# Four graph-attention layers on one core: columns W times a by VectorE, rows R by transfers, the mask without GpSimd

## The chip, the core and the metric

The kernel runs on one core of a Trainium2 chip. The core has five engines with queues of their own: TensorE (PE, with PEld for its weight loads), VectorE (DVE), ScalarE (ACT), GpSimd (POOL) and SyncE (SP), which here only issues transfers (DMA). They share the on-chip memory SBUF; PE writes to eight accumulator banks, the PSUM. An engine runs its queue in order. Where an instruction needs what another engine or a transfer makes, it waits on a semaphore. The metric is the device time of one execution in microseconds, as the median over runs.

## The reference

Input are x of 32 batches x 512 nodes x 256 features, an adjacency matrix adj of 512 x 512 shared by all batches, and the weights of four layers. Each layer adds to x the output of a graph attention over `h = relu(layernorm(x))`. The core of each is

```python
Wh = h @ W
s_i, s_j = Wh @ a1, Wh @ a2
e = leaky_relu(s_i[:, :, None] + s_j[:, None, :], alpha)
e = where(mask, e, -inf)
out = act(softmax(e, axis=-1) @ Wh)
```

Layers 0 and 1 have one head of 256 features (alpha 0.2 and 0.01, then elu or relu); layer 0's mask is `(adj > 0) | eye`. Layer 2 has four heads of 64. Layer 3 is a chain: a linear map from 256 to 512 with relu, an attention over all nodes without a mask (W_fc, 512 features), two elus and a residual, a linear map back to 256, and a masked attention (W_hand) with a residual.

## The kernel before

**The algebra.** With `s = s_i + s_j`, exp(leaky_relu(s)) is max(exp(s), exp(alpha s)). After division by a factor that depends on i alone, which the softmax cancels, the weight of pair (i, j) is exp(s_j) times max(r_i, t_j). r and t are exponentials of the projections scaled by 1 - alpha and alpha - 1. So each weight matrix W gets three more columns: W times a2, and two scaled copies of W times a2 and a1. One product `hT x W` then makes the values and the three exponents. `values` (L669) scales the values by exp(s_j) and leaves the three exponentials in the columns F, F + 1 and F + 2 of v. `weights` (L704) makes w, with j on the partitions and i along the free axis: `max(R, t_j) * maskT`. R is r spread over all partitions: every partition holds the same row r_i, i = 0..511. `averages` multiplies w with v on PE; column F gives the denominator.

**R.** `weights` has two sources for R. By default (L709 to L711), PE makes it: for each of the four tiles of 128 nodes, it turns the column of r, repeated 128 times, against the identity, which leaves R in a PSUM bank. If the caller gives `r`, this is used instead. Layer 2 does that: `rows_out` (L721) turns the four columns of all tiles in one go, ScalarE copies them to an SBUF tile `row`, a transfer puts them into DRAM, and `spread` (L731) reads each row back into all 128 partitions, into one of three buffers `spread`. The sort of layer 3 (`sort_attend`) takes its row in the same way. Layers 0 and 1 and the second attention of layer 3 call `plain` (L749), which uses the default.

**Masked and unmasked attention.** The unmasked attention of layer 3 (`sort_attend`) needs no 512 x 512 weights: nodes are placed in order of t by indirect transfers, running sums are made, and each node gathers the sums at its place. Only the last batch uses the direct form, `attend`.

**Set-up.** x of the first four batches, adj, and all weights come in by transfers from SP. `fetch_w` loads a W with room for three columns, `fetch_a` loads a with one element per partition. `finish_w` then makes the three columns of each 128 rows of W with `project` (L474): PE turns the blocks of W, ScalarE copies them, PE multiplies them with a, VectorE copies the result into W. W0 is done first; the others come from `setup` (L568), a generator, whose steps are placed between those of the first batches. `setup` also makes the mask: VectorE compares adj with 0 into `own`, GpSimd sets the diagonal to 1 with `affine_select` (L572), PE turns the blocks, ScalarE copies them into maskT.

**Order.** The 32 batches run as four streams of eight batches each. Each stream is a Python generator that yields after each piece of work the time at which it wants its next turn (`after_us`); LEAD is the distance between the streams' starts. The order of these turns gives the instructions their ranks. The program is then built twice. The first build is rehearsed: `jobs_of` and `price` give every instruction a duration and `in_order` (L251) lets the engines and SP's queue pick the ready instruction of the lowest rank at every moment. The second build fixes the order found for each engine (`arrange`) and the PSUM banks. So the numbers given to `after_us` are no waits on the chip: they only shift what comes before what.

Of the kernel before, what the change touches and what calls it, by code (L numbers as in the profile page):

```python
# [30 lines left out]
P = 128  # L31
# [36 lines left out]
class Job:  # L68

    def __init__(self, place, ins):  # L70
        self.place, self.ins = place, ins
        self.engine, self.op = str(ins.engine).split(".")[-1], ins.opcode
        self.real, self.soft = set(), set()
        self.after, self.behind, self.opens, self.uses = [], [], [], set()
        self.ready, self.left, self.led, self.rank = 0.0, 0, False, place
# [34 lines left out]
def price(job, outs, ins, in_psum):  # L110

    e, op = job.engine, job.op
    if op == "Matmult":
        (name, _, moving), (_, _, still) = ins[0], ins[1]
        job.span = int(job.ins.tile_size[1])
        turned = name.startswith("ident")
        whole = str(list(job.ins.ins)[1].dtype).endswith("float32")
# [8 lines left out]
    if op == "DMACopy":  # L126
# [6 lines left out]
        if kind == "x" and ins[0][1] == 0:  # L133
            job.took = 5000.0
# [116 lines left out]
def in_order(jobs, users, homes):  # L251
# [27 lines left out]
    array = {"load": 0.0, "flow": 0.0, "end": 0.0, "span": P, "idle": 0.0, "last": 0.0}  # L279
# [23 lines left out]
    def put(job, e, at):  # L303
# [21 lines left out]
        else:  # L325
            clock[e], done = at + job.holds, at + job.took
        array["last"] = max(array["last"], done)
# [71 lines left out]
def fast(ctx, tc, plan, flag, x, adj, w0, a0, w1, a1, w2, a2, mlp1_w, mlp1_b, mlp2_w, mlp2_b,  # L399
# [10 lines left out]
    LEAD = 75.63  # L410
    SLOW = 1.43
    STRETCH = 1.5
# [61 lines left out]
    def project(dst, block, k, a_cols):  # L474
# [12 lines left out]
        nc.vector.tensor_copy(dst, q[:, :n] if len(dst.shape) == 2 else q[:, :n].rearrange("p (h c) -> p h c", c=3))  # L487

    def fetch_w(w, a, name):
# [6 lines left out]
        return t, fetch_a(a, name + "a") if len(a.shape) == 2 else a  # L496

    def finish_w(fetched, alpha):
        t, a_cols = fetched
# [9 lines left out]


    a0_sb = fetch_a(a0, "W0a")
    xts = {0: load_x(0)}
    W0, _ = fetched0 = fetch_w(w0, a0_sb, "W0")
# [4 lines left out]
    W1, _ = fetched1 = fetch_w(w1, a1, "W1")  # L518
# [4 lines left out]
    A2 = const.tile([P, KF, NH * 3], FP, name="A2")  # L523
    nc.vector.memset(A2, 0.0)
    for h in range(NH):
        t, r = divmod(h * D, P)
        for s, c in ((0, 2), (1, 0)):
            nc.sync.dma_start(
                A2[r:r + D, t, h * 3 + c:h * 3 + c + 1],
                a2[h:h + 1, s * D:(s + 1) * D].rearrange("o d -> d o"),  # L530
            )
    A2v = A2.rearrange("p k (h c) -> p (k h) c", c=3)
    WM1 = const.tile([P, KF, H], FP, name="WM1")
    nc.sync.dma_start(WM1, mlp1_w.rearrange("(k p) f -> p k f", p=P))
    WFC, _ = fetched3 = fetch_w(w_fc, a_fc, "WFC")
    WM2 = const.tile([P, KH, F], FP, name="WM2")
    nc.sync.dma_start(WM2, mlp2_w.rearrange("(k p) f -> p k f", p=P))
    WHA, _ = fetched4 = fetch_w(w_hand, a_hand, "WHA")
# [8 lines left out]
    C = F + 2  # L547
# [6 lines left out]
    for _ in finish_w(fetched0, 0.2):  # L554
        pass
# [12 lines left out]
    def setup():  # L568
# [3 lines left out]
        nc.gpsimd.affine_select(  # L572
            out=own, in_=own, pattern=[[P, NT], [-1, N]], base=0, channel_multiplier=1,
            compare_op=OP.not_equal, fill=1.0,
        )
        nc.vector.tensor_reduce(differ[:, 0:1], adj_sb, AX.XY, OP.min)
        nc.vector.tensor_scalar(differ[:, 0:1], differ[:, 0:1], 0.0, None, op0=OP.is_lt)
        for j in range(NT):
# [3 lines left out]
            nc.scalar.copy(maskT[:, j, :], p)  # L582
        yield
        yield from finish_w(fetched1, 0.01)


# [4 lines left out]
        nc.vector.tensor_scalar_mul(A2v[:, :, 1:2], A2v[:, :, 0:1], -0.8)  # L591
        nc.vector.tensor_scalar_mul(A2v[:, :, 2:3], A2v[:, :, 2:3], 0.8)
        for k in range(KF):
            project(W2[:, k, :, D:], lambda k, f: raw2[:, k, f * P:(f + 1) * P], k, A2)
            yield
        yield from finish_w(fetched3, 0.2)
# [17 lines left out]
        yield from finish_w(fetched4, 0.2)  # L614
# [38 lines left out]
    def turned(xn, when):  # L653
# [5 lines left out]
        yield after_us(2.12)  # L659
# [9 lines left out]
    def values(hT, w, rs=None):  # L669

        v = work.tile([P, NT, F + 3], FP, tag="v", name="v", bufs=4)
        for t in range(NT):
# [14 lines left out]
            if t + 1 < NT:  # L687
                yield after_us(0.72)
        yield after_us(0.03)
        return v  # L690

    def linear_t(inT, w, bias, name, bufs):
# [3 lines left out]
        for f in range(ft):  # L696
# [4 lines left out]
            yield after_us(0.76 if f == ft - 1 else 1.59)  # L701
# [47 lines left out]
    def plain(hT, w, rs=None):  # L749
        v = yield from values(hT, w, rs)  # L750
        wt = weights(lambda t: v[:, t, F + 2:F + 3], lambda j: v[:, j, F + 1:F + 2])
        note(v[:, :, F:])
        yield after_us(4.32)
# [19 lines left out]
    def layer0(xt, xn, rs, when):  # L773
        v, wt = yield from plain((yield from turned(xn, when)), W0)
        xn, rs = new_xn(), small([NT], "rs")
        for t0 in range(0, NT, 2):
            r, q = pair(), pair("q")
            for i in range(2):
# [3 lines left out]
                if i == 0:  # L782
                    yield after_us(2.78)
            add_elu(xt[:, t0:t0 + 2, :], r, q)
            norm(xt, xn, rs, t0, True)
            last, when = when, after_us(1.15)
            if t0 == 0:
                yield after_us(5.01)
# [3 lines left out]
    def layer1(xt, xn, rs, when):  # L792
        v, wt = yield from plain((yield from turned(xn, when)), W1, rs)
        xn, rs = new_xn(), small([NT], "rs")
        for t0 in range(0, NT, 2):
            r = pair()
            for i in range(2):
                p, rd = averages(v, wt, t0 + i)
                nc.scalar.activation(r[:, i, :], p, AF.Relu, scale=rd)
                if i == 0:  # L800
                    yield after_us(2.38)
# [3 lines left out]
            last, when = when, after_us(4.67)  # L805
            if t0 == 0:
                yield after_us(12.63)
# [3 lines left out]
    def layer2(xt, xn, rs, when):  # L811
        hT = yield from turned(xn, when)
        v = work.tile([P, NT, NH, CH], FP, tag="v", name="v2", bufs=4)
        for t in range(NT):
# [11 lines left out]
            yield after_us(0.87 if t + 1 < NT else 0.62)  # L826
# [4 lines left out]
        def begin():  # L831
# [4 lines left out]
            return after_us(1.36)  # L836
# [7 lines left out]
        yield after_us(9.98)  # L844
        begin()
        note(v.rearrange("p t h c -> p (t h) c")[:, :, D:])
        yield after_us(7.5)
        when = begin()
        for g, parts in enumerate(plan):
# [10 lines left out]
            yield after_us(0.16)  # L860
# [29 lines left out]
            yield after_us(0.3)  # L890
# [3 lines left out]
        yield after_us(9.4)  # L894
        return xn, rs, after_us(1.32)
# [28 lines left out]
    def attend(oT, b):  # L924

        halves, ends = fc_values()
        for c in range(2):
            for t in range(NT):
                project_half(oT, halves, ends, c, t)
                yield after_us(0.3)  # L930
# [4 lines left out]
        yield after_us(0)  # L935
        ys = []
        for t in range(NT):
# [10 lines left out]
            yield after_us(0.16)  # L948
            if t:
                mlp_in(oT, ys[t - 1], t - 1)  # L950
                yield after_us(0.3)
        yield after_us(3.15)
        mlp_in(oT, ys[-1], NT - 1)
        yield after_us(2.72)

    def sort_attend(oT, b):
# [6 lines left out]
        for t in range(NT):  # L963
            project_half(oT, halves, ends, 0, t)
            yield after_us(0.49)
        project_half(oT, halves, ends, 1, 0)
        yield after_us(0.06)
# [3 lines left out]
        yield after_us(0.73)  # L971
# [10 lines left out]
        sort = after_us(16.48)  # L982
        yield after_us(7.62)
        for t in range(1, NT):
            project_half(oT, halves, ends, 1, t)
            yield after_us(1.52)
# [7 lines left out]
        for c in range(2):  # L994
# [17 lines left out]
            sort = after_us(1.66)  # L1012
        places = table[:N, :].rearrange("(p t) (k c n) -> p (t k) c n", t=NT, k=2, c=2)
        sort = after_us(6.05)
        for c in range(2):
# [15 lines left out]
            yield after_us(3.52)  # L1031
# [602 lines left out]
```

## Time and profile before

| what | value |
|---|---|
| median of 11 runs | 2784.43 us (2781.42 to 2793.45) |
| the profiled execution | 2787.69 us, its span 2785.8 us |
| busy PE / DVE / ACT / POOL | 2742.5 / 2272.2 / 1635.5 / 521.4 us |
| mean granted clock of PE | 0.994 of full speed |
| transfers | 287.37 MB, mean 103 GB/s |
| issues of `spread<-row` and `row<-row` | 159 of 256 KB and 63 of 2 or 8 KB |
| turns `b<-ident,v` | 416 (384 of them for R, 32 for layer 2's rows) |

A line of the page such as `L714 DVE SCALAR_TENSOR_TENSOR w<-spread,v,maskT` names the source line, the engine, the operation, and what it writes and reads by the program's names; `b` is a PSUM bank, `spread` the SBUF buffer of R. In a fp32 product PE needs two instructions; a turn against the identity needs one. In a timeline, the first number is the start in us from the span's beginning, the second the length of the merged group, and the bracket gives the idle time before it and what ended it.

### The profile page before, as it was taken

The numbers are of one execution on the slowest core, as the hardware profiler recorded it, in microseconds if no ns is written. First come the engines' busy times: TensorE is split into PE (matmuls) and PEld (weight loads), VectorE is DVE, ScalarE is ACT, GpSimd is POOL, SyncE is SP. The second block draws the span as 40 slices with busy tenths as digits, with TensorE's granted clock in tenths as the row PEclk, the third lists the DMA queues.
The fourth block names the chain that finished last, engine by engine and source line by source line (L and its number), as shares of the span: only waits on it lengthen the run. The fifth ranks groups of instructions, "written<-read, shape, count | busy, mean of one in ns | idle before, by whom it ended". The sixth has DMA issues, their size and how long they took to land.

```text
span 2785.8 us, 41668 instructions
## 1 busy us (share of the span) xinstructions
PE 2742.5 (98%) x14316; PEld 1953.9 (70%) x14316; DVE 2272.2 (82%) x5834; ACT 1635.5 (59%) x4142; POOL 521.4 (19%) x515
## 2 busy tenths in 40 slices
PE   7999999999999999999999999999999999999998
PEld 6676676767766677766866667776676766867665
DVE  4779887897978879788796888978888897888964
ACT  3455666556655666556655566655666555655555
POOL 0012221121202222022211222111221122211220
PEclk8999999999999999999999999999999999999999
DMA  3024341343413434134331433223432233422430
GB/s 99 16 75 135 108 141 65 98 136 98 149 51 111 137 107 134 35 123 130 116 117 52 132 120 124 92 69 115 130 118 89 84 127 103 141 80 84 134 118 32
DMA packets 202499, 287.37 MB, mean 103 GB/s; under 512 B 18156, under 2 KB 157350, under 8 KB 202280
## 3 DMA queue, kind: packets, MB, share of 16 engines
q1 hardware_dynamic: 172520, 186.34, 21.4%
q0 software_dynamic: 29760, 98.30, 10.5%
q8 instruction: 114, 1.87, 0.3%
q14 instruction: 105, 0.86, 0.1%
HBM read 169.14 MB, written 115.45 MB: 102 GB/s over the span
## 4 chain that ended last, share of the span: by engine, by line
PE 88%; DVE 4%; issue 4%; DMA 2%; ACT 1%; POOL 1%; SPq 0%; POOLq 0%; ACTq 0%
PE b L430 66%; PE b L434 12%; PE b L438 10%; DMA spread<-row 1%; DVE st L630 0%; DVE w L714 0%; DVE y L771 0%; DMA row<-row 0%; DVE xn L637 0%; DMA W<-in_L_gnn_W_dram 0%; POOL order L998 0%; DVE y L1107 0%; DVE y L764 0%; DMA g<-table,at 0%; DVE q L769 0%
## 5 line engine op out<-in xcount | busy, mean ns | idle before, releaser
L430 PE MATMUL b<-v,w 128*128 128x257 f32 (+1 forms) x3136 | 767.7, 383 | 2.1 <-DVE w L718 1.0
L430 PEld LDWEIGHTS b<-v,w 128*128 128x128 f32 x3136 | 573.4, 191 | 123.1 <-issue 34.2
L430 PE MATMUL b<-WFC,oT 128*128 128x256 f32 (+1 forms) x2048 | 490.5, 381 | 1.0 <-ACT oT L700 1.0
L430 PEld LDWEIGHTS b<-WFC,oT 128*128 128x128 f32 x2048 | 374.2, 189 | 75.2 <-issue 18.6
L430 PE MATMUL b<-W,hT 128*128 128x259 f32 (+1 forms) x1536 | 397.3, 389 | 0.5 <-ACT hT L651 0.5
L714 DVE SCALAR_TENSOR_TENSOR w<-spread,v,maskT 128x512 f32<-128x512 f32 x512 | 373.1, 778 | 13.6 <-PE b L434 13.1
L434 PE MATMUL b<-w,v 128*32 128x512 f32 x3072 | 349.4, 595 | 0.0
L998 POOL DMA_INDIRECT order<-v,at x248 | 262.2, 1057 | 411.4 <-DVE at L980 147.0
L430 PEld LDWEIGHTS b<-W,hT 128*128 128x128 f32 x1536 | 280.0, 192 | 61.8 <-issue 22.7
L714 DVE SCALAR_TENSOR_TENSOR w<-b,v,maskT 128x512 f32<-128x512 f32 x384 | 264.7, 743 | 21.9 <-PE b L438 19.6
L1110 POOL TENSOR_TENSOR x<-x,y 128x512 f32<-128x512 f32 x62 | 82.4, 1328 | 1030.9 <-ACT y L1108 1021.7
L1052 POOL DMA_INDIRECT g<-table,at x124 | 139.7, 1127 | 568.2 <-DMA table<-sums 270.6
L430 PE MATMUL b<-hT,WM 128*128 128x512 f32 x512 | 243.6, 592 | 0.4 <-ACT hT L651 0.4
L434 PEld LDWEIGHTS b<-w,v 128*32 128x32 f32 x3072 | 89.8, 109 | 198.2 <-issue 195.6
L430 PE MATMUL b<-oT,WM 128*128 128x512 f32 x512 | 227.5, 592 | 0.0
L630 DVE BATCH_NORM_STATS2 st<-x 128x6 f32<-128x256 f32 x512 | 194.3, 408 | 4.9 <-DMA x<-in_x_dram 3.6
L651 ACT ACTIVATE hT<-b 128x512 f32<-128x512 f32 x256 | 147.6, 593 | 45.1 <-PE b L438 45.1
L746 DVE RECIPROCAL rden<-b 128x1 f32<-128x1 f32 x388 | 57.7, 160 | 137.5 <-PE b L430 134.9
L430 PEld LDWEIGHTS b<-oT,WM 128*128 128x128 f32 x512 | 97.1, 190 | 102.8 <-issue 100.0
L438 PE MATMUL b<-ident,xn 128*128 128x128 f32 x1024 | 158.2, 276 | 8.2 <-DVE xn L637 8.2
L771 DVE TENSOR_TENSOR y<-q,y 128x512 f32<-128x512 f32 (+1 forms) x194 | 132.5, 683 | 33.1 <-ACT q L770 31.9
L922 ACT ACTIVATE v<-b,ends 128x256 f32<-128x256 f32 x256 | 120.6, 471 | 62.9 <-PE b L430 50.4
(154 smaller groups left out, 4237.1 us busy)
## 6 DMA issues: line engine op xcount, KB each, us to landing
table<-sums SPq DMA_DIRECT2D x62, 1032.0 KB
spread<-row SPq DMA_DIRECT2D x159, 256.0 KB
sums<-order SPq DMA_DIRECT2D x62, 516.0 KB
x<-in_x_dram SPq DMA_DIRECT2D x32, 512.0 KB
out_dram<-x SPq DMA_DIRECT2D x62, 256.0 KB
sums<-order SPq DMA_DIRECT2D x62, 129.0 KB
order<-v,at POOLq DMA_INDIRECT x248, 2.7
g<-table,at POOLq DMA_INDIRECT x124, 5.0
```

Of the source, the lines that this page charges most:

```text
L430: nc.tensor.matmul(p, w, x, **flags)
L434: nc.tensor.matmul(p, w, x, tile_position=(0, c), **flags)
L438: nc.tensor.transpose(p, x, i)
L630: nc.vector.bn_stats(st[:, i, :], xt[:, t0 + i, :])
L651: nc.scalar.activation(hT[:, :, t0 * P:(t0 + 2) * P], p.rearrange("p (k n) -> p k n", k=KF), AF.Relu)
L714: nc.vector.scalar_tensor_tensor(wt[:, j, :], r, t_col(j), maskT[:, j, :], op0=OP.max, op1=OP.mult)
L746: nc.vector.reciprocal(r, den)
L771: nc.vector.tensor_tensor(r, q, r, op=OP.add)
L922: nc.scalar.activation(halves[c][:, t, :F], ps[:, :F], AF.Copy, scale=ends[:, t, 0:1])
L998: one = nc.gpsimd.indirect_dma_start(out=orders[c], out_offset=bass.IndirectOffsetOnAxis(ap=at[:, 0, t:t + 1], axis=0), in_=halves[c][:, t ...
L1052: nc.gpsimd.indirect_dma_start(out=g, out_offset=None, in_=table, in_offset=bass.IndirectOffsetOnAxis(ap=at[:, 1, t:t + 1], axis=0),)
L1110: (nc.gpsimd if n == 2 else nc.vector).tensor_tensor(xr, xr, y, op=OP.add)
```

## The change

Four things change together.

1. Columns W times a. W0 keeps `finish_w`. For W1, WFC and WHA, a is spread over all partitions by one transfer each (`fetch_row`), and VectorE multiplies each row of W with it and adds up along the row (`finish_by_rows`); the scaling of two of the columns is done on GpSimd on W's own columns. W2 gets its columns by a product and a reduction per head. The transfers of single elements of a1, a2, a_fc and a_hand go, and the order of the first transfers becomes x, W0, a0, adj.
2. R. `plain` gets `far`; layers 0, 1 and layer 3's second attention make R with `rows_out` and `spread`, as layer 2 does, from column F + 2 of v.
3. The mask. `affine_select` goes. After each bank of turned blocks is copied to maskT, VectorE writes the diagonal block once more as the maximum of the turned block and the identity.
4. The order. `price` and `in_order` treat the first loads as sharing one pipe (`flux`), and turns no longer count as a switch of PE's tile size. LEAD, SLOW, STRETCH and nearly all times given to `after_us` are new, PAUSES adds pauses after layers 0 to 2 of each stream's first batch, and the steps of `setup` are placed 19.61 apart and not 1.5.

```diff
-        job.span = int(job.ins.tile_size[1])
         turned = name.startswith("ident")
+        job.span = P if turned else int(job.ins.tile_size[1])
...
-        if kind == "x" and ins[0][1] == 0:
-            job.took = 5000.0
+        if ins[0][0].startswith("in_") and not (kind == "x" and ins[0][1] >= 4 * 512 * 256):
+            job.took, job.flux = 2500.0, max(160.0, 4.0 * elements(s) * s[0][1] / 350.0)
...
-    LEAD = 75.63
-    SLOW = 1.43
-    STRETCH = 1.5
+    LEAD = 81.69
+    GO = 7.0
+    PAUSES = (1.98, 20.79, 0, 9.87, 13.42, 5.98, 12.87, 2.43, 0, 28.8, 13.7, 0)
+    SLOW = 1.53
+    STRETCH = 1.75
...
+    def finish_by_rows(t, row, alpha):
+
+        kt, halves = t.shape[1], row.shape[1] // (2 * F)
+        for k in range(kt):
+            dots = work.tile([P, 2, 2], FP, tag="T", name="dots", bufs=2 * NS)
+            for s, c in ((0, 2), (1, 0)):
+                for i in range(halves):
+                    at = (s * halves + i) * F
+                    junk = work.tile([P, N], BF, tag="junk", name="junk0", bufs=1)[:, :F]
+                    nc.vector.scalar_tensor_tensor(
+                        junk, t[:, k, i * (F + 3):i * (F + 3) + F], 1.0, row[:, at:at + F], op0=OP.mult, op1=OP.mult,
+                        accum_out=t[:, k, F + c:F + c + 1] if halves == 1 else dots[:, s, i:i + 1],
+                    )
+                if halves > 1:
+                    nc.vector.tensor_tensor(t[:, k, F + c:F + c + 1], dots[:, s, 0:1], dots[:, s, 1:2], op=OP.add)
+            yield
+        scale_a(t[:, :, F:F + 3], alpha)
...
+    def fetch_row(a, dst):
+        nc.sync.dma_start(dst, a.partition_broadcast(P))
+        return dst
...
-    for h in range(NH):
-        t, r = divmod(h * D, P)
-        for s, c in ((0, 2), (1, 0)):
-            nc.sync.dma_start(
-                A2[r:r + D, t, h * 3 + c:h * 3 + c + 1],
-                a2[h:h + 1, s * D:(s + 1) * D].rearrange("o d -> d o"),
-            )
...
         nc.vector.tensor_scalar(own, adj_sb, 0.0, None, op0=OP.is_gt)
-        nc.gpsimd.affine_select(
-            out=own, in_=own, pattern=[[P, NT], [-1, N]], base=0, channel_multiplier=1,
-            compare_op=OP.not_equal, fill=1.0,
-        )
...
             nc.scalar.copy(maskT[:, j, :], p)
+            nc.vector.tensor_tensor(maskT[:, j, j * P:(j + 1) * P], p[:, j * P:(j + 1) * P], ident, op=OP.max)
...
-    def plain(hT, w, rs=None):
+    def plain(hT, w, rs=None, far=False):
         v = yield from values(hT, w, rs)
-        wt = weights(lambda t: v[:, t, F + 2:F + 3], lambda j: v[:, j, F + 1:F + 2])
+        r = None
+        if far:
+            r = spread(rows_out(v[:, :, F + 2], 1)[0, :])
+            yield after_us(11.34)
+        wt = weights(lambda t: v[:, t, F + 2:F + 3], lambda j: v[:, j, F + 1:F + 2], r=r)
         note(v[:, :, F:])
-        yield after_us(4.32)
+        yield after_us(0.41)
...
-    ready = {i: i * LEAD + late for i, late in enumerate((0, -2.47, -0.73, -8.03))}
+    ready = {i: i * LEAD + late for i, late in enumerate((0, 4.35, 4.97, 5.59))}
...
-    ready[NS] = 0.35
+    ready[NS] = 1.42
...
-            ready[i] += 1.5
+            ready[i] += 19.61
```

## The prediction

> **What bounds the kernel now.** I read the page's busy shares first, then busy time by stretch, then PE's timeline, and the chain of waits last. The page and two stretches (columns: length, then busy time of PE, PEld, DVE, ACT, POOL, PE's clock, DMA share, GB/s):
>
> ```profile
> PE 2742.5 (98%) x14316; PEld 1953.9 (70%) x14316; DVE 2272.2 (82%) x5834; ACT 1635.5 (59%) x4142; POOL 521.4 (19%) x515
> ...
> PE 88%; DVE 4%; issue 4%; DMA 2%; ACT 1%; POOL 1%; SPq 0%; POOLq 0%; ACTq 0%
> ```
>
> ```profile
> 0.00:60.00 60.00, 40.12 (x190) 34.05 (x191) 22.92 (x78) 20.11 (x51) 5.71 (x18) 0.83 0.40 115
> ...
> 516.29:853.42 337.13, 336.97 (x1770) 239.86 (x1769) 284.06 (x728) 203.38 (x517) 66.38 (x65) 1.00 0.34 108
> ```
>
> From 516.29 on, the program repeats every 337.13 us, one round of four batches, and PE is busy for 336.97 of it. So a round is worth what PE's own instructions take, and no wait of another engine shows. Room lies only in the first 60 us (PE busy 40, clock 0.83) and in the end (PE's last instruction starts at 2777.1 of 2785.8).
>
> PE's timeline, start and length. Lengths overlap, so I take the distance between starts:
>
> ```profile
> 1025.80 0.60 PE L438 MATMUL b<-ident,v 128*128 128x128 f32 x4
> 1026.23 0.60 PE L438 MATMUL b<-ident,rT 128*128 128x128 f32 x4
> ...
> 1034.07 0.27 PE L438 MATMUL b<-ident,ends 128*4 128x128 f32 x1
> 1034.18 1.90 PE L430 MATMUL b<-v,w 128*128 128x257 f32 x8
> ```
>
> The first row is what the change removes: the four turns that make R, 0.43 us, 0.109 each. The third is what it puts there: one turn of a few columns, 0.11. The same view of the start:
>
> ```profile
> 6.98 0.66 PE L438 MATMUL b<-ident,W 128*128 128x128 f32 x2 [6.98 <-DMA W<-in_L_gnn_W_dram]
> ...
> 19.46 2.82 PE L438 MATMUL b<-ident,own 128*128 128x128 f32 x12 [4.21 <-POOL own L572]
> ...
> 30.38 0.44 PE L438 MATMUL b<-ident,raw 128*128 128x128 f32 x2 [2.30 <-DVE W L487]
> 30.65 0.60 PE L438 MATMUL b<-ident,v 128*128 128x128 f32 x4
> ...
> 32.10 2.08 PE L430 MATMUL b<-v,w 128*128 128x257 f32 x4
> ...
> 53.97 1.11 PE L438 MATMUL b<-ident,xn 128*128 128x128 f32 x4 [3.84 <-DVE xn L637]
> ```
>
> At present R is ready for VectorE within 32.10 - 30.65 = 1.45 us of its first turn. The price of R by transfers is in the chain of waits, where the sort's own row takes this way:
>
> ```profile
> 359.94 0.25 ACT row L726
> 360.19 0.02 issue
> 360.20 2.75 DMA row<-row
> 362.96 0.02 issue
> 362.97 4.90 DMA spread<-row
> ```
>
> **The change part by part.** The sum is made against the profiled execution: span 2785.8, 2787.69 in all, 3.3 above the median 2784.43 (0.12%). I take the difference and put it on the median. A measurement of this kernel can tell about 0.2% (5.6 us) from no change.
>
> (a) R of layers 0 and 1 and of layer 3's second attention. Each of 32 batches loses 3 x 4 turns and gains 3 x 1: 32 x 9 x 0.109 = 31.4 us of PE. PE bounds the rounds, so this is worth all of it, if nothing else stops PE: -31.4.
>
> (b) Columns W times a. On PE, the turns and small products of W1, raw2, WFC and WHA stand between 23.80 and 50.13. By distances of starts: W1 1.55, raw2 with A 1.80, WFC 5.95, WHA 1.63, together -10.9. VectorE gets them: 24 products of 128x256 with accumulation (as 128x258, 484 ns, and an accumulator read, 84) and 4 pairs of about 0.84 us, 17 us. VectorE is busy 22.9 of the first 60 us, so most lies in its idle time.
>
> (c) Waits that go. The mask no longer passes POOL, and `own` no longer stands behind the copy of raw2 on VectorE's queue: adj is there by about 9.6 (issue 2.88, own transfer some 6.7), and the walk below has PE reach `own` with no gap: 4.21. The 2.30 before raw2's turns go with these turns, as does 0.52 before WHA's last product. x and W0 are issued before the 256 single elements of each half of a0, W0 at 1.3 and not at 2.33: 1.0. Together -8.0. The four `max` on the diagonal blocks (0.3 us each) run beside PE's next turns. SP loses 14 of its small early issues and gains four spreads of a.
>
> (d) What the first R costs. In the changed program's order PE has nothing between stream 0's turn of r and its first average: cover 0.11 us. Walk: PE starts at 5.95; the W0 steps and xn's turns end at about 12.2 (as 6.98 to 13.20 now); values and `own`, about 9 us at a clock partly halved, end near 21; ACT's last scaling and the turn, 22.5. But SP issues in order, and the row stands behind all weights and an x of 512 KB. SP's issues that wait for x1, x2 and x3 stand at 11.4, 12.6 and 14.1 now: 1.35 us for 512 KB. After x3 come 3.75 MB up to WHA, 10 to 11 us, so WHA lands near 25, and the row waits for its semaphore. Row 2.75, spread 4.0 to 4.9, first w 0.74: averages begin near 33.5, against 32.10 now. PE waits some 11 us there, then starts at half clock: the four products at 32.10 took 2.08 now, 0.87 at full rate. No setup stands between them, so the averages end near 43, and layer 1's values near 56, against 61.5. Its R has a cover of 3.7 us, need about 6.8 to 8.4, so PE waits 3 to 5 more and layer 1's averages begin at 64 to 66, against 63.74, with 3 us more of stream 1 done. Of the 19.6 us that (b), (c) and two R's save by then, some 18 are given back: +18 (12 to 24).
>
> (e) The rest of the run-in, to 265. Stream 1's first R has a cover of 3.6 and hides behind the wait before it; layer 2's four rows 8.6, which must bring two heads (VectorE 4 x 0.744 for the first); the others 8.3 to 15.6. The lower bound is no loss, the upper 2 us for each of five: +4 (0 to 10).
>
> (f) The rounds. By the changed order and the row prices, PE's cover from each turn of r to the first product that needs it is 9.28, 9.28, 9.50, 10.09 and so on to 13.18 us, twelve in a round. The need: 0.5 to 1 until ACT's copy, 0.25, row 1.2 to 4, spread 3 to 4.9 (the chain showed 2.75 + 4.90 and, at 2046, 3.72 + 4.04), first w 0.74: 6 to 9.7, plus VectorE's queue. Mostly hidden; +4 over all rounds, bounds 0 and 30 (a third of a microsecond for each of 84 steady R's). SP gets 12 rows and 12 spreads more per round, 24 issues of about 0.35 us beside some 75, and 3.1 MB beside 36: it can be held up, not filled. ACT gets 12 copies of 0.25.
>
> Now w is made from SBUF and not from PSUM; the tile's view:
>
> ```profile
> L714 DVE SCALAR_TENSOR_TENSOR w<-spread,v,maskT x512: 720/744/2142, 98.7 to 2651.2; 128x512 f32<-128x512 f32 x171
> L714 DVE SCALAR_TENSOR_TENSOR w<-b,v,maskT x384: 727/743/752, 31.3 to 2769.8; 128x512 f32<-128x512 f32 x192
> ```
>
> The medians are equal; only the SBUF form has a tail (mean 778 against 743), so 384 x 35 ns = 13.4 us more on VectorE, 1.7 in a round where it idles 53: nothing on the path. The Trainium skill speaks against this part: "GPSIMD Engine Reference", section Specifications, says that GpSimd's SBUF interfaces are shared with VectorE, with contention where an instruction has two SBUF inputs, which this form has and the PSUM form has not. By that rule, the 62 additions of x on POOL (1328 ns each) could each hold one w up to the tail's 1.4 us: an estimate of 87 us of VectorE at the worst, 11 in a round, still inside its 53. The sum stays as the rows have it.
>
> A second page prices (f) otherwise. "DMA: Bandwidth & Descriptors", section Anatomy of one DMA, gives some 2.0 us plus bytes over 436 GB/s for a transfer, fitted on GpSimd's path: an estimate of 4.6 us for row and spread together, which would make (f) zero and the forecast 4 us lower. The chain measured 7.65 and 7.76 us for the two, and I keep to that.
>
> (g) The end. The last two R's have covers of 7.1 and 7.9 against some 6.8; PE's gaps there come from layer chains that stay: +1 (-2 to +5).
>
> Sum: -31.4 - 10.9 - 8.0 + 18 + 4 + 4 + 1 = -23.3, so 2784.4 - 23.3 = 2761.
>
> **The rivals.** 1. All covered: (d) at 12, the rest nothing, -38, 2746. For it: the rounds of now, where each R by transfer in layer 2 is waited for by nobody. Against: those have more work in between, and the first R is plainly uncovered. 2. A longer run-in: (d) and (e) at their upper ends and (g) at 5 give -7.3, 2777, and one more stretch at half clock (6.8 us in the records) 2784. For it: 53.97 above, where one wait is followed by PE at half clock. 3. Slower: R by transfers becomes the rounds' bound. If transfers take so much longer that the chain from turn to w takes 10.7 us, the four shortest covers lack 4.6 us per round, 32 over seven, and 4 of these are in (f): 2789. That is the point from which it decides; at 12 us eight covers lack 13 per round, 92 in all: 2849. Against: 9.7 is the worst sum of the rows shown. For it: SP's order, where a row waits behind whatever stands before it. 4. VectorE as the bound: 284 + 2 in a round of 333 is 86%, no bound by itself.
>
> **How the numbers follow.** Forecast (2750 to 2771) 0.60; rival 1 0.18; rival 2 0.13, of which half ends within 0.2%; rival 3 and 4 together 0.09. Faster by over 0.2% is 0.60 + 0.18 + half of rival 2, 0.85; within 0.2% 0.07; slower 0.08, the rest of 3 being a draw. The range runs from rival 1's lower edge to where rival 2 ends: 2742 to 2783.
>
> **What would show it.** Right: a round of about 333.2 with PE busy but for 0.5; no turns b<-ident,v of 128 columns; no PE wait on POOL own; a PE gap of about 10 us near 22 to 33, ended by DVE w, with SP's row issue at 25 or later; stream 0's layer 1 averages at 63 to 66. Wrong: (f), if PE's gaps in a round end on DVE w behind DMA spread; (d), if the row goes out well before 25, or if PE's waits sit elsewhere; (a), if the turns' time comes back as gaps.

## The result and the profile after

The changed kernel takes 2767.0 us (median of 8 runs, 2762.41 to 2770.82) against 2784.45 us of the kernel before beside it: a ratio of 0.9935, 95% interval 0.9926 to 0.9943. It is 17.4 us faster; 23.3 were forecast. The profiled execution has a span of 2766.3 us, 19.5 less than before's 2785.8.

The page of the changed kernel, busy time and the chain that ended last:

```profile
PE 2708.6 (98%) x13944; PEld 1908.4 (69%) x13944; DVE 2290.4 (83%) x5889; ACT 1627.3 (59%) x4228; POOL 517.1 (19%) x516
...
PE 68%; DVE 24%; ACT 5%; issue 1%; DMA 1%; SPq 0%; POOL 0%; DVEq 0%; POOLq 0%
```

PE is still busy for 98%, but the chain of waits that ended last now runs through VectorE for a quarter of the span, where it was 4%. That is a warning more than a loss: PE and VectorE now hand work to each other with little in hand, as the run with a longer way for the row shows below.

The first 60 us and one round, by stretch (columns as before):

```profile
0.00:60.00 60.00, 34.09 (x133) 27.59 (x134) 33.92 (x133) 20.38 (x57) 4.04 (x16) 0.80 0.45 143
785.72:1120.54 334.82, 334.03 (x1734) 235.36 (x1733) 285.21 (x730) 203.03 (x529) 65.33 (x64) 1.00 0.37 118
```

A round went from 337.13 to 334.82 us, with PE busy for all but 0.8 of it. In the first 60 us PE does less (34 us and not 40), partly because work was removed, partly because it waits. PE's timeline shows where:

```profile
19.54 0.27 PE L442 MATMUL b<-ident,v 128*4 128x128 f32 x1 [0.26 <-ACT v L703]
33.60 10.21 PE L434 MATMUL b<-v,w 128*128 128x257 f32 x32 [13.79 <-DVE w L737]
...
48.73 0.66 PE L442 MATMUL b<-ident,xn 128*128 128x128 f32 x2 [3.55 <-ACT rs L656]
```

The single turn of r ends at 19.8, and the first average starts 13.79 us later. The chain of waits through that gap (start, length, what):

```profile
16.47 9.25 DMA WHA<-in_L_gnn_W_hand_dram
...
25.79 3.54 DMA row<-row
29.33 0.02 issue
29.35 3.42 DMA spread<-row
32.77 0.02 issue
32.79 0.76 DVE w L737
```

ScalarE had copied the row by 20.1. It went out only at 25.79, when a load issued long before it, WHA of layer 3, had landed.

### The profile page after: what moved, and what is told of

It is laid out like the page before. It is cut to its first block, busy times and chain, and to the rows that moved or that the text cites. A ratio compares the mean times of both kernels' runs of the same rounds, so it can differ in the third digit from the quotient of the medians.

```text
span 2766.3 us, 41413 instructions
## 1 busy us (share of the span) xinstructions
PE 2708.6 (98%) x13944; PEld 1908.4 (69%) x13944; DVE 2290.4 (83%) x5889; ACT 1627.3 (59%) x4228; POOL 517.1 (19%) x516
## 4 chain that ended last, share of the span: by engine, by line
PE 68%; DVE 24%; ACT 5%; issue 1%; DMA 1%; SPq 0%; POOL 0%; DVEq 0%; POOLq 0%
PE b L434 54%; PE b L438 7%; DVE w L737 7%; PE b L442 7%; DVE st L653 2%; DVE sums L1055 1%; DVE y L798 1%; DVE sums L1070 1%; DVE xn L664 1%; ACT q L797 1%; DVE xn L660 1%; DVE y L1134 1%; DVE sums L1063 1%; DVE y L791 1%; DVE g L1093 1%
## 5 line engine op out<-in xcount | busy, mean ns | idle before, releaser
L434 PEld LDWEIGHTS b<-v,w 128*128 128x128 f32 x3136 | 579.2, 191 | 145.1 <-issue 30.6
L737 DVE SCALAR_TENSOR_TENSOR w<-spread,v,maskT 128x512 f32<-128x512 f32 x896 | 652.8, 761 | 26.3 <-DMA spread<-row 25.7
L434 PE MATMUL b<-WFC,oT 128*128 128x256 f32 (+1 forms) x2048 | 504.7, 381 | 0.0
L434 PE MATMUL b<-W,hT 128*128 128x259 f32 (+1 forms) x1536 | 386.1, 388 | 0.8 <-ACT hT L674 0.8
L442 PE MATMUL b<-ident,xn 128*128 128x128 f32 x1024 | 161.8, 279 | 12.4 <-DVE xn L660 6.8
L442 PEld LDWEIGHTS b<-ident,xn 128*128 128x128 f32 x1024 | 122.7, 141 | 62.1 <-DVE xn L660 13.5
L1137 POOL TENSOR_TENSOR x<-x,y 128x512 f32<-128x512 f32 x62 | 86.1, 1388 | 357.5 <-ACT y L1135 355.1
```

The costliest lines, as they stand in the source:

```text
L434: nc.tensor.matmul(p, w, x, **flags)
L442: nc.tensor.transpose(p, x, i)
L737: nc.vector.scalar_tensor_tensor(wt[:, j, :], r, t_col(j), maskT[:, j, :], op0=OP.max, op1=OP.mult)
L1137: (nc.gpsimd if n == 2 else nc.vector).tensor_tensor(xr, xr, y, op=OP.add)
```

## The experiments

Two notes on reading. Chips fall into two levels: on some the kernel before takes 2784 us, on others 2815 to 2817. Every ratio is therefore to the kernel before on the same chip, and differences are told within one level. And a kernel's order is written anew for every edit, since it is found by a rehearsal of the whole program; an edit in one place can move instructions everywhere.

Theory 1: R by transfers earns the gain in the rounds, and the run-in gives part of it back. Theory 2: R by transfers brings new small waits through VectorE into every round. Theory 3: the gain is that of the set-up, or of the order, and R adds nothing.

| kernel | median us | before, same chip | ratio, 95% interval |
|---|---|---|---|
| order and set-up new, R by turns | 2813.87 | 2814.87 | 0.9995 (0.9983 to 1.0006) |
| set-up alone | 2811.28 | 2814.87 | 0.9983 (0.9972 to 0.9994) |
| order alone | 2814.00 | 2814.87 | 0.9994 (0.9983 to 1.0005) |
| changed kernel, second level | 2772.40 | 2817.07 | 0.9839 (0.9822 to 0.9855) |
| kernel before, profiled there | 2816.76 | 2817.07 | 0.9998 (0.9988 to 1.0007) |
| R by transfers alone | 3103.09 | 2817.07 | 1.1013 (1.0995 to 1.1032) |
| first batch's R by turns | 2953.46 | 2817.07 | 1.0483 (1.0464 to 1.0502) |
| changed kernel, first level again | 2762.45 | 2783.81 | 0.9919 (0.9905 to 0.9932) |
| R's row by a longer way | 2817.76 | 2783.81 | 1.0122 (1.0107 to 1.0138) |
| first R a constant | 2757.56 | 2783.81 | 0.9905 (0.9890 to 0.9921) |
| late loads behind the first row | 2757.82 | 2783.81 | 0.9904 (0.9889 to 0.9920) |
| all of layer 3's loads behind it | 2777.12 | 2817.18 | 0.9854 (0.9841 to 0.9868) |

### One part at a time: set-up, order, both without R

The first kernel is the changed one with R made by PE again:

```diff
-        v, wt = yield from plain((yield from turned(xn, when)), W0, far=True)
+        v, wt = yield from plain((yield from turned(xn, when)), W0)
```

(the same for W1 and WHA).

> The changed kernel, but R of layers 0, 1 and layer 3's second attention made on PE by turns again; the rest of the change, the new order times included, stays. Theory 1 (R by transfers takes 3.93 us per round off PE and gives about 20 us back in the run-in; the 1.6 us of small PE waits that a round of the changed kernel has belong to the new order times, not to R): rounds of 334.82 + 3.93 = 338.7 us, PE's wait of 13.8 us near 20 gone, total 2767 + 31.4 - 20 = 2778. Theory 2 (the small waits come with R by transfers, through VectorE): rounds of 337.1, total 2767 to 2769. Theory 3 (the gain is of the set-up alone and R by transfers gains nothing net): total 2767 or less.

The second is the kernel before with parts 1 and 3 of the change and the new sequence of loads, but R by turns and the old times; the third is the kernel before with part 4 alone.

> The kernel before with the new set-up alone (columns W times a on VectorE, spread a, mask without GpSimd, new order of the first loads); R by turns and the order times of before. Theory 1: rounds stay at 337.1; the run-in saves PE's 10.9 us of set-up and 8.0 us of waits, most of it on the path because nothing now waits for R: 2784.4 - 15 = 2769 (2765 to 2775). Theory 3: the same 2767 as the whole change. If the set-up were hidden by streams anyway: 2780 to 2784.

> The kernel before with the new order alone (prices of first loads and turns, LEAD, PAUSES, all times given to after_us); set-up and R as before. Theory 1 (the small PE waits of 1.6 us per round come with the new order): rounds of 338.5 to 338.8, total 2784 + 11 = 2795 or a little more in the run-in. Theory 2 (they come with R by transfers): rounds of 337.1, total 2782 to 2790. If the new order is itself better: below 2780.

Against the kernel before they measured -1.0, -3.6 and -0.9 us, on a chip of the second level. None brings the gain, nor do set-up and order together, so theory 3 falls there; on the first level the three were not run. The set-up takes 9.3 us of full-speed work off PE and three waits, and 3.6 came out: in its start PE waits 9.03 us at 25 us for the first w and 3.70 for `own`. The kernel with set-up and order but R by turns has later rounds of 338.9 us on average (theory 1 had 338.7), with 1.9 us of PE waits in each; the changed kernel on a chip of this level (next section) has 1.0. The small waits are thus no smaller without R by transfers, which speaks against theory 2; each order has its own.

### The changed kernel and the kernel before on a chip of the second level

> The changed kernel once more, beside the runs below on one chip. Theory 1 (R by transfers earns the gain, about 3.9 us of every round of four streams, and the run-in gives some 9 back): about 17 us below the kernel before, as measured first (2767.0 against 2784.4), whatever the level of the chip. Theory 3 (set-up or order earn it, and R by transfers is paid for by new waits): on a chip where set-up alone was worth 3.6 us and order with set-up 1.0, no more than some 5 us below.

> The kernel before, profiled on this chip, to hold its rounds against those of the runs beside it. Same time as the kernel before; rounds of 337.1 us if the chip is as the first one; if the level is 30 us higher as with the last three runs, the difference should be found in the rounds (about 4 us in each) as slips of ScalarE and VectorE with a half-speed clock window, not in TensorE's work.

The gain is 44.7 us there, not 17.4. From the first kernel above (-1.0, on another chip of this level) to the changed one (-44.7) only R changes, and the order that follows from it. The turns explain 31.4 of this; the rest is not settled to the microsecond, since the orders differ and the changed kernel's profiled run (2782.14) was the slowest of its four.

Why is the gain larger there? The kernel before loses time in each round at one place. PE's one long wait in a round on this chip, and the chain that leads to it in the same round (start, length, what):

```profile
PE b L430 <- DVE oT L1125: 2.4, 1, 2.4
```

```profile
924.32 0.60 DVE y L764
924.92 2.88 another core or an unknown queue
927.81 0.02 issue
927.83 0.70 DVE oT L1125
```

ScalarE stands still over the same time (2.63 us before `v<-b,ends`, L922), also released by something that the profile doesn't name. On the first chip the same two instructions follow with no gap. This costs 2.4 us of PE's time per round, and its rounds are 340.8 to 342.4 us where they were 337.13. The changed order has this wait once (3.61 us from 239.55) and not in the later rounds, which are 335.8 us on average. What releases the two engines late on such chips stays open; indirect transfers of GpSimd are under way there, and nothing was tried on them.

### R by transfers alone

```diff
+        if far:
+            r = spread(rows_out(v[:, :, F + 2], 1)[0, :])
+            yield after_us(20.0)
```

with `far=True` in the three calls, in the kernel before. (The pause is 20.0 and not the change's 11.34: with that one and the other times of before, the three buffers of R allowed no order, and no kernel came of it.)

> The kernel before with R by transfers alone: set-up, mask and all order times of before, except that the order's pause between the row's transfer and the weights is 20.0 us. The turns give 3.9 us in each round. Its order leaves some R's in each round only 1.6, 4.6 and 6.6 us between their last turn and the first use, others 16 and more, where the chain of row and spread took 10 us. Theory 1: waits of about 8, 6 and 4 us per round take the gain and more: rounds about 8 to 14 us longer, some 60 to 100 us above the kernel before. Rival (the hidden transfers are shorter in a round than in the run-in, or the wait falls on VectorE only): within 20 us of the kernel before.

It is 286 us slower, 10%. One round, PE's waits in a round, and PE's timeline at the largest:

```profile
1045.62:1424.60 378.98, 351.12 (x1740) 242.04 (x1739) 288.48 (x736) 205.35 (x532) 67.38 (x64) 0.96 0.34 106
```

```profile
PE b L430 <- DVE w L714: 7.8, 4, 6.8
PE b L438 <- DVE y L775: 6.1, 5, 2.6
PE b L430 <- ACT y L1101: 3.2, 1, 3.2
PE b L438 <- DVE xn L641: 2.7, 3, 1.6
```

```profile
1173.14 0.27 PE L438 MATMUL b<-ident,v 128*4 128x128 f32 x1
1180.18 8.64 PE L430 MATMUL b<-v,w 128*128 128x257 f32 x30 [6.78 <-DVE w L714]
```

The last turn of r stands right in front of the averages, so 6.78 us of its chain lie bare. That is the wait that theory 1 foresaw, but the waits for w are only 7.8 us of a round. Waits on y, xn and oT make up more than half of the 29.7 us of waits per round, and 28.2 us of each round run at half clock (the 0.96), which costs 14 more. 29.7 + 14.1 - 4.0 for the turns is 39.8; the round is 41.8 longer than the 337.13 of the first chip. The expected 60 to 100 us counted the bare R's alone. It missed that the four streams had moved: their distances at the same step are 54, 65, 65 and 196 us in this kernel, and 68, 72, 65 and 137 in the kernel before. That these distances cause the other waits is likely, but no run tests it. So taking the turns off PE gains nothing by itself: it depends on the order. The run does not price R by transfers in the old order, because that order was not kept.

### The first batch's R by turns

```diff
-    def layer0(xt, xn, rs, when):
-        v, wt = yield from plain((yield from turned(xn, when)), W0, far=True)
+    def layer0(xt, xn, rs, when, far):
+        v, wt = yield from plain((yield from turned(xn, when)), W0, far=far)
```

with `far` true from batch 1 on, and the same for layer 1.

> The changed kernel, with R of the first batch's layers 0 and 1 by turns on TensorE as before; all the rest as changed. 64 turns come back on TensorE (64 by 0.109 us, 7.0 us), and the first wait of TensorE for w (13.8 us, with a clock window of 17.1 us at half speed behind it, some 8 us lost) loses its cause. Theory 1, in which the run-in's waits for R cost 18 us: 13.8 + 1.2 + up to 8 less 7.0, so 8 to 16 us below the changed kernel. Rival: the run-in is bound by the start-up chain of VectorE and ScalarE that stands behind the wait (xn, rs, the masks), so that other gaps take its place: within 4 us of the changed kernel, either way.

Both expectations were wrong: 136 us above the kernel before, some 181 above the changed one. The 13.79 us wait is gone, but PE waits 41.6 us in the run-in in all (39.6 in the changed kernel on this chip), in smaller pieces: 3.78 on rs, 2.37 on xn, 5.76 on w, 4.22 on xn. The streams then stand 76, 83, 90 and 107 us apart, where the changed kernel has 79, 71, 110 and 75, and later rounds take 353 to 361 us. So the edit changed the whole order, and this run does not price the first wait; a later one does. A stretch of one, with PE's clock in the third number from the end, and the instruction in front of it:

```profile
1047.70:1061.40 13.70, 10.52 (x28) 7.19 (x29) 8.06 (x22) 8.48 (x18) 1.92 (x2) 0.50 0.39 116
```

```profile
1047.79 1.11 PE L442 MATMUL b<-ident,y 128*128 128x128 f32 x4 [2.98 <-issue]
```

A wait of 2.98 us is followed by 13.7 us at half clock, in which two more waits lie, of 1.39 and 1.17 us. The Trainium skill, "TensorE: Matmul & The Clock Gate", section "HAM oscillation — how this bites in real kernels", gives as the rule that PE should have no idle gap above some 3.4 us. This case disagrees in the unsafe direction: 2.98 was enough here, and waits of 1.6 to 2.2 us were enough in the kernel of the last section. It was not certain either: of eight waits of 2.4 us in the kernel before on this chip, three were followed by a half-speed window of 3.4 us and five by none. A wait of 3.7 us near 89 us in the changed kernel was followed by such a window on two chips and by none on a third.

### R's row by a longer way

```diff
-            r = spread(rows_out(v[:, :, F + 2], 1)[0, :])
+            near = rows_out(v[:, :, F + 2], 1)
+            way = dram.tile([1, N], FP, tag="way", name="way", bufs=4)
+            nc.sync.dma_start(way, near)
+            r = spread(way[0, :])
```

The rehearsal prices the added transfer at nothing, so the order on PE, VectorE and ScalarE is that of the changed kernel. This and the next two kernels ran beside the changed kernel on a chip of the first level.

> The changed kernel, but R's row of layers 0, 1 and the hand layer goes through DRAM once more (a 2 KB transfer from DRAM to DRAM between row and spread); the order on TensorE, VectorE and ScalarE is that of the changed kernel. A row transfer took 1.14 to 4.3 us, so each of the 96 chains, 7.2 us long in the middle and 9.8 in the longest tenth, grows by about 2 us. Theory 1 (R is hidden in the rounds, but with covers of only 9.3 to 13.2 us, so with 1 to 3 us in hand): the three waits of the run-in grow by 2 each, and the longest chains of a round overrun the shortest covers by up to 2.5 us in one to three places: 10 to 40 us above the changed kernel, with new TensorE waits that end on w. Rival (the covers counted in TensorE's work understate what is in hand): no wait for w in the rounds, 3 to 7 us above it from the run-in alone.

> The changed kernel, for comparison on the same chip: 17 us (as measured first) to 45 us (as measured on the second chip) below the kernel before.

The kernel is 55.3 us slower than the changed one beside it (2817.76 against 2762.45): more than the 10 to 40 of theory 1, and far more than the rival's 3 to 7. PE's longest waits over three rounds, here and then in the changed kernel beside it:

```profile
PE b L434 <- DVE w L737: 8.6, 8, 2.2
PE b L442 <- ACT y L889: 1.2, 3, 0.5
```

```profile
PE b L442 <- DVE xn L660: 1.0, 3, 0.3
PE b L442 <- DVE y L798: 0.3, 1, 0.3
```

These three rounds take 1026.1 us against 1004.1. Of the 22.0 us, 8.6 are the waits for w, of which the changed kernel has none in a round; 6.9 are averages that start one by one, as w comes; the rest is in smaller waits and slips. VectorE waits for a spread nine times in a round, and not three. The run-in is 6.7 us longer, with PE's first two waits for w at 15.48 and 3.00 us for 12.11 and 1.27. So the rival falls, and theory 1 has the place right and the price too low: R is hidden in the rounds with less in hand than one more small transfer takes (from its issue to the spread's, this one took 1.9 us in the middle of 96). The prediction's third rival had 4.6 us per round if the chain took 10.7 us and 13 if it took 12; this run lies between.

### The price of the first wait

```diff
-            r = spread(rows_out(v[:, :, F + 2], 1)[0, :])
+            row = rows_out(v[:, :, F + 2], 1)[0, :]
+            if begin:
+                r = work.tile([P, N], FP, tag="spread", name="first", bufs=3)
+                nc.gpsimd.memset(begin.pop() and r, 1.0)
+            else:
+                r = spread(row)
```

The rehearsal is told that this tile comes when the spread would, so PE, ScalarE and GpSimd keep their order. R of batch 0's layer 0 is left out of the computation.

> The changed kernel with its order on every engine kept, but R of batch 0's layer 0 is a constant tile, set at the start by GpSimd, instead of the row's values (so this R is left out of what is computed, and one spread transfer with it). Prices the first wait of TensorE (13.8 us, end at 33.6) by itself. VectorE then reaches the first w after the products that wait for the last layer's vector (landed at 23.5), near 25.1 in place of 32.8. Theory 1 (the wait and the half clock behind it are lost time, the 18 us of the prediction): the wait shrinks to 5 to 7 us, the half clock's 17.1 us to 10.2 or less, and the kernel is 7 to 12 us below the changed kernel. Rival (the wait covers the start-up of VectorE and ScalarE, which would end the next waits instead): within 3 us of it.

It measured 4.9 us below the changed kernel (2757.56 against 2762.45; each ratio is known to about 4 us): between theory 1 (7 to 12) and the rival (within 3). The traces show more. PE's first averages, in the changed kernel beside it and here:

```profile
33.50 9.42 PE L434 MATMUL b<-v,w 128*128 128x257 f32 x32 [12.11 <-DVE w L737]
```

```profile
26.89 9.08 PE L436 MATMUL b<-v,w 128*128 128x257 f32 x32 [5.29 <-DVE w L739]
```

The wait falls from 12.11 to 5.29 us; what is left of it is VectorE's products for W_fc, which stand before w and wait for a vector until 24.65. The half clock behind it falls from 13.7 to 6.8 us. At the end of the run-in, taken at stream 3's first layer 2 row (the turn of 16 columns), this kernel is at 266.25 us and the changed one at 275.22. So 9.0 us were lost time, as theory 1 has it, and no other gap took their place; the later rounds are alike (334.8 and 334.7 us). The spans of the two profiled executions differ by 7.7 us; the medians do not settle the rest.

### A mend: loads behind the first row

In `price`, loads that are needed late are held back in SP's order until the first spread is issued: WM1, WM2, WHA with its vector, two biases and the diagonal of adj (seven; the expectation's nine is a miscount), batch 4's x and the two fills.

```diff
+        if (ins[0][0].startswith(("in_L3_gnn_mlp2","in_L3_gnn_W_hand","in_L3_gnn_a_hand","in_L3_gnn_mlp1_b"))) or name.startswith("diag") or ins[0][0].startswith("zero") or (kind == "x" and ins[0][1] == 4 * 512 * 256) or ins[0][0].startswith(("in_L3_gnn_mlp1")):
+            job.ready = 19500.0
```

> The changed kernel with nine start-up loads that only layer 3 needs, the load of batch 4's x and two fills of a table with zeros issued behind the first row and spread on SyncE's queue, not ahead of them; the order on TensorE and ScalarE is unchanged. In the changed kernel the row was ready at 20.1 us and issued at 25.8, behind those loads, and took 3.5 us to land, spread 3.4. Theory 1: row issued near 20.2, spread landed near 26, w 5 to 7 us earlier; 4 to 10 us below the changed kernel, so the best of both. Rival (the loads were not what held the row, or their delay stops VectorE's products or layer 3 of the first stream at 85 us): within 2 us of it, or above.

It measured 2757.82 (2754.07 to 2758.87), 4.6 us below the changed kernel beside it (2757.90 to 2766.69). It is the fastest complete kernel on this level, as expected of theory 1, but the two intervals to the kernel before (0.9889 to 0.9920 and 0.9905 to 0.9932) overlap, so for the whole time this is likely and not shown. The run-in is shown by the traces. The chain of waits and PE's first averages:

```profile
19.58 1.18 DMA row<-row
...
20.82 4.35 DMA spread<-row
...
25.20 0.76 DVE w L739
```

```profile
26.00 10.18 PE L436 MATMUL b<-v,w 128*128 128x257 f32 x32 [6.77 <-DVE w L739]
```

The first w comes at 25.20 us where the changed kernel beside it has 32.69, PE's first wait is 6.77 for 12.11, the half clock behind it 10.2 for 13.7, and stream 3's first layer 2 row stands at 268.97 for 275.22: the run-in keeps 6.2 us.

The last kernel holds back every load of layer 3 (names that begin with `in_L3`; nine, where the expectation counts eleven) and x of batch 4:

> As the run before with the loads behind (4.6 us below the changed kernel on one chip), but all eleven loads of layer 3's weights, vectors and biases and batch 4's x stand behind the first row and spread; the diagonal of adj and the zeros are issued early again. Nothing is then in flight when the row is issued at some 20.2 us, so row and spread should take the 1.2 and 3.0 us of the shortest ones (3.5 and 3.4 in the changed kernel): spread landed near 25, first w near 25 in place of 32.8, TensorE's first wait some 6 us in place of 13.8. Theory 1 (the first wait is lost time, with the half clock behind it): 6 to 11 us below the changed kernel (0.988 to 0.990 of the kernel before on a chip like the first). Rival (VectorE's products of W_fc, which now come later, and the start-up of VectorE and ScalarE take the place of the wait): no more than 5 us below the changed kernel, with other gaps in the first 100 us.

The chain of waits and PE's timeline at its start:

```profile
20.25 1.14 DMA row<-row
...
21.45 4.56 DMA spread<-row
...
26.04 0.76 DVE w L739
```

```profile
26.84 9.64 PE L436 MATMUL b<-v,w 128*128 128x257 f32 x32 [6.93 <-DVE w L739]
```

The row goes out at 20.25 instead of 25.79 and lands after 1.14 us instead of 3.54: SP's earlier loads were what held it. The spread takes 4.56 and not the 3.0 expected, with the held-back loads issued right behind it. PE's first wait is 6.93 instead of 13.79, the half clock behind it 10.2 instead of 17.1 us, and stream 3's first layer 2 row comes at 277.23, where the changed kernel on a chip of this level has 284.31. So the run-in keeps 7.1 us. The time does not show it: 0.9854 against the changed kernel's 0.9839, with overlapping intervals. They are different chips, and its rounds are 0.3 us longer; which part is the chip's is open.

## Why the prediction was right, step by step

PE has 316 turns and 56 small products of the set-up fewer. At their full-speed distances (0.109 and 0.112 us from start to start) they are 40.7 us of work. With all of PE's instructions priced in this way, what a stretch takes beyond that work grew by 11.1 us in the run-in (to the first layer 2 row of stream 3), by 6.7 in the rounds and 3.4 at the end. The sum is the -19.5 of the spans.

**(a) R's turns, -31.4: right.** The turns `b<-ident,v` fell from 416 to 128, and PE's starts that belong to R fell from 5.26 to 1.23 us per round, 4.03 where 3.93 were forecast. R is also what the gain depends on: without it, set-up and order are worth 1 us on a chip of the second level.

**(b) Columns off PE, -10.9: a little too much.** 40.7 - 31.4 leaves 9.3 us of full-speed work. Some of the distances it was read from lay at half clock (32.1 to 38.9 us). That part was not work, and the changed kernel has as much half clock and more in its run-in.

**(c), (d), (e) The run-in: right in sum, and in its mechanism almost to the microsecond.** `own` is reached without a wait; row issue "at 25 or later" was 25.79; averages at 33.5 were at 33.60; the gap "of about 10 us" was 13.79, since the turn came at 19.5 and not 22.5. That the averages were met to 0.1 us is part luck: the row took 3.54 us for 2.75, and the spread 3.42 for 4.0 to 4.9. Layer 1's averages came earlier, 62.21 for 64 to 66, with a wait of 1.20 for the 3 to 5. (c) + (d) + (e), less the 1.6 that (b) had too much, make +12.4 for the 11.1 measured. The kernels with loads behind the row show that the 25.79 was SP's queue of loads and not ScalarE or R itself, and that half of the first wait could go; the constant R shows that the wait and its half clock were time lost.

**(f) The rounds, +4: the term that was mis-sized.** The round was forecast at 333.2 and took 334.82. The missing 1.6 us is no wait for R, which is what (f) had priced: no PE wait in a steady round ends on w. PE's waits over three rounds, after, then before:

```profile
PE b L442 <- DVE xn L660: 1.0, 3, 0.3
PE b L442 <- ACT y L1124: 0.6, 3, 0.2
PE b L442 <- ACT y L886: 0.2, 1, 0.2
```

```profile
PE b L438 <- DVE xn L637: 0.5, 3, 0.2
```

With smaller ones these are 0.8 us per round against 0.2. Most of the rest are turns of xn started one by one, as VectorE and ScalarE bring them, at some 50 ns more each: 15 per round and not 2, 0.8 us. Seven rounds make 11 us of it; before's last rounds (337.7 and 340.1) were longer too, so 6.7 remain. The 4 was near the 6.7 by luck: it priced another wait. Transfers were priced from 7.65 and 7.76 us, two chains from the upper end: over 159 pairs in the changed kernel, row and spread took 4.15 to 8.55 us, 4.97 in the middle and 7.44 at nine tenths. The estimate from "DMA: Bandwidth & Descriptors", 4.6 us, is near the middle; but covers must hold the upper end, and the longer way shows that they do so with less in hand than one more such step.

**w from SBUF.** The tile's view after:

```profile
L737 DVE SCALAR_TENSOR_TENSOR w<-spread,v,maskT x896: 718/746/1777, 32.8 to 2749.4; 128x512 f32<-128x512 f32 x180
```

The 13.4 us did not come: added up one by one, all w took 682.1 us for 683.6 before. (VectorE's busy time on w rose from 637.8 to 652.8 us, since fewer of them follow each other without a gap.) The forecast had carried the tail over to the 384 new ones, but only 15 of the 896 took over 820 ns, as many as of the 512 before. Each of them overlaps one of GpSimd's additions of x (L1137). So what "GPSIMD Engine Reference", Specifications, says of the shared interface is seen here, up to 1 us at a time, but 15 times and not the 62 of the estimate, and no PE wait in a steady round ends on w.

**(g) The end, +1:** 3.4, with two new waits on w (1.13 and 0.55 us, from 2737.95 and 2748.70), inside the stated -2 to +5.

The rivals: the longer run-in did not come, the bound on R's transfers did not either, but it was closer than the 0.09 given to it suggests: one more small transfer brings PE's waits for w into every round.

## What to carry to other kernels

A product removed from a bound engine pays only if the order hides what replaced it. On chips of one level, the whole change with R by transfers gave -44.7 us in an order found for it, and R by transfers alone gave +286 in another. Before trusting a latency as hidden, lengthen it by one small step with the order kept, and measure; the price tells what is in hand. In a run-in, ask what stands in the queue ahead of the first latency-critical transfer: a row of 2 KB waited 5.7 us behind loads for layer 3, which begins after 85 us.

## What the runs showed of the hardware

- The kernel before takes 1.1% longer on some chips than on others with the same program. In the profiles most of it goes with one place per round where ScalarE and VectorE stand still for 2.6 to 2.9 us on a release that the profile doesn't name.
- PE's clock halved after waits of 1.6 to 3.0 us, and after equal waits of 2.4 and 3.7 us it sometimes did not. With clusters of such waits, 28 of the 379 us of a round ran at half speed.
- A 2 KB row took 1.14 us with nothing else in flight (DMA share 0.00 in the 2.25 us before it) and 3.54 behind loads; a 256 KB spread took 4.56 us with loads issued right behind it, and 3.42 behind the last of them.
